# Cross-attention in seven-product blocks: product 2 of y, itself made by seven smaller products

## The chip, the cores and the metric

The kernel runs on one NeuronCore of one Trainium2 chip. The metric is the device time of one execution in microseconds (us). Matmuls run on TensorE (PE; its weight loads are recorded apart, as PEld), elementwise work on VectorE (DVE) and ScalarE (ACT), reductions over partitions on GpSimd (POOL). SyncE (SP) only issues DMAs, ACT and POOL issue a few. Each engine works through its own instructions in their order; where one needs the result of another engine, it waits on a semaphore.

## What is computed

For each of 8 batches, with C = 512 channels, N = 1024 positions and D = 64, all in float32:

```python
q = jnp.einsum('bcn,dc->bnd', x1, Wq) + bq
k = jnp.einsum('bcn,dc->bdn', x2, Wk) + bk[:, None]
v = jnp.einsum('bcn,dc->bdn', x2, Wv) + bv[:, None]
attn = jax.nn.softmax(jnp.einsum('bnd,bdm->bnm', q, k), axis=2)
attn_out = jnp.einsum('bcm,bnm->bcn', v, attn)
return attn_out + x1
```

`x1` is `x` (8, 512, 1024) and `x2` is `ctx_2048` of the same shape.

## The kernel before

Let e be the exponentials of the scores, 1024 (m) by 1024 (n), not yet divided by their sums. The kernel computes y = x2 e (512 by 1024) divided by the sums of the columns, and then out = Wv y + bv + x1. Both products are made from 2 by 2 blocks with the seven-product form of block multiplication (Winograd's variant of Strassen's): seven block products for eight, at the price of sums and differences of blocks. Blocks of the left factor (x2 transposed, called `a`, or the weights `w`) are `11`, `12`, `21`, `22`, with the sums S1 to S4; blocks of the right factor (`e`, called `t`, or `y`) have the sums T1 to T4. `MULT` (line 270) says for each product which left and right blocks it takes, into which pair of PSUM banks (`a` or `c`) it goes, and whether it opens them; otherwise it adds to what is there. Partial sums that are needed alone are copied out of PSUM by ACT into `tmp` on the way (products 1, 6, 5).

`multiply` (line 280) makes one block product. For y it is two halves j of 128 rows, each of four matmuls (contraction 4 x 128) with a moving operand of 128x512. A float32 matmul shows in the trace as two MATMUL and two LDWEIGHTS instructions, so such a product is 16 MATMULs. For out (`second`) a block product has half the contraction: 8 MATMULs.

`period` (line 442) is one batch `s` and, woven into it, the preparation of the next one, `n`. The order of the work is written out by hand; each engine follows the order of this code. PE's order in a period is: first(1), first(2), first(6) for y; the scores of the first half of `n` and the projection to queries; first(5), first(7), first(3); the scores of the second half of `n` and the keys; first(4); and then second(1), (6), (2), (5), (7), (3), (4) for out.

DVE has, among others, these steps in a period:

- `sum_e` "T1", "T2", "T4", "T3" (line 256): differences of blocks of e, each in two steps of 128x1024 elements. T3 is written in place, T4 has a buffer of its own (`eT4`).
- `evict_y` "11", step 1 (line 305): adds product 2 in bank pair `c` to the copy of product 1.
- `sums` (line 345): adds up e over the rows of blocks; `total` (line 215) then has POOL reduce it over partitions to `den`; two small DMAs and a reciprocal in `shares` (line 224) turn it into the factors for y.
- `fold` "max", `highest`, `exponentials` (lines 197, 210, 238): maximum over the scores of `n`, subtraction, and ACT's Exp.
- `sum_a` (line 127): S1 to S4 of `n`. S4 = `12` - S2 is made after first(3) of `s` (line 512); in the first period all four are made at the end of the period (lines 539 and 546).
- `evict_o` (line 330): adds bias, x1 and copies to the products of out, and SP sends the tile away.

The buffers: `a12`, `a11`, the S tiles, both e tiles and the T tiles are single; `a21` and `a22` are double. `load_a` (line 120) issues the loads of the blocks of `n` from SP, in the order of the code with all other loads and stores of SP. In PSUM there are the four banks `a0`, `a1`, `c0`, `c1`, and two double banks `sc` for scores and projections; the third of four scores uses bank pair `c` (first half) or `a` (second half).

In the first period (`s.b == 0`) things lie otherwise: the second half of the exponentials of batch 1 is made after first(1), and T4 after first(2).

Of the kernel before, what the change touches and what calls it, by code (L numbers as in the profile page):

```python
# [9 lines left out]
F32 = mybir.dt.float32  # L10
AF = mybir.ActivationFunctionType
ALU = mybir.AluOpType
# [3 lines left out]
def kernel(  # L16
# [8 lines left out]
    bv: bass.AP,  # L25
    out: bass.AP,
):

# [26 lines left out]
    nc = tc.nc  # L57
    P = 128
# [3 lines left out]
    H = 512  # L62
    MH = N // P // 2
# [4 lines left out]
    sb = ctx.enter_context(tc.tile_pool(name="sb", bufs=1))  # L68
# [3 lines left out]
    ps_s = ctx.enter_context(  # L72
        tc.tile_pool(name="ps_s", bufs=2, space=bass.MemoryType.PSUM)
    )
    ps_a = ctx.enter_context(
        tc.tile_pool(name="ps_a", bufs=1, space=bass.MemoryType.PSUM)
    )
# [6 lines left out]
    w = {  # L84
        k: const.tile([P, 2, C // 2], F32, name=f"w_{k}")
        for k in ("11", "12", "21", "22", "S1", "S2", "S4")
    }
# [6 lines left out]
    def left_sums(a, *ks):  # L94

        for k in ks:
            x, y, op = {
                "S1": ("21", "22", ALU.add),
                "S2": ("S1", "11", ALU.subtract),
                "S3": ("11", "21", ALU.subtract),  # L100
                "S4": ("12", "S2", ALU.subtract),
            }[k]
            nc.vector.tensor_tensor(a["21" if k == "S3" else k], a[x], a[y], op)  # L103
            if k == "S3":
                a["S3"] = a["21"]

    class Batch:
        def __init__(self, b):
            self.b = b
            self.a, self.e, self.t, self.y, self.o = {}, {}, {}, {}, {}  # L110
            self.mx, self.top, self.den, self.few, self.rden = {}, {}, {}, {}, {}
            self.tmp, self.bank = {}, {}

    def load_x(s, x):

        s.x = sb.tile([P, CT, N], F32, tag="x", name=f"x_{s.b}_{x.tensor.name}")
        for c in range(CT):
            nc.sync.dma_start(s.x[:, c, :], x[s.b, ts(c, P), :])  # L118
# [8 lines left out]
    def sum_a(s, *ks):  # L127
        for k in ks:
            if k != "S3":
                s.a[k] = sb.tile([P, MH, C // 2], F32, tag=f"a{k}", name=f"a{k}_{s.b}")  # L130
        left_sums(s.a, *ks)

    def project(s, nm, w_sb, bank=None):

        if bank:
            ps = ps_a.tile([P, H], F32, tag=bank, name=f"ps_{nm}_{s.b}")
        else:
            ps = ps_s.tile([P, 2, H], F32, tag="sc", name=f"ps_{nm}_{s.b}")[:, 0, :]
        for c in range(CT):
            for h, r in ((0, lo), (1, hi)):  # L140
                nc.tensor.matmul(  # L141
                    ps[r, :],
                    w_sb[:, c, :],
                    s.x[:, c, ts(h, H)],
                    start=(c == 0),
                    stop=(c == CT - 1),
                )
        return ps
# [12 lines left out]
    def keys(s, bank=None):  # L161

        ps = project(s, "k", wk_sb, bank)
        s.k = sb.tile([P, H], F32, tag="k", name=f"k_{s.b}", bufs=2)
        nc.scalar.activation(s.k, ps, AF.Identity, bias=bk_sb)  # L165
# [58 lines left out]
    def shares(s, h):  # L224

        nc.vector.reciprocal(s.few[h], s.few[h])  # L226
        row = dram.tile([1, H], F32, tag="row", name=f"row_{s.b}_{h}")
        nc.gpsimd.dma_start(row.rearrange("o (p f) -> (o p) f", p=P), s.few[h])
        s.rden[h] = s.den[h]
        nc.gpsimd.dma_start(s.rden[h], row.broadcast_to([P, H]))  # L230
# [16 lines left out]
        nc.vector.tensor_tensor(t[k], t[x], t[y], ALU.subtract)  # L247

    def open_t(s):
        for n in ("T1", "T2", "T4"):  # L250
            s.t[n] = sb.tile([P, MH, H], F32, tag=f"e{n}", name=f"e{n}_{s.b}")
        e0, e1 = s.e[0], s.e[1]
        s.t |= {"11": e0[:, 0], "12": e1[:, 0], "21": e0[:, 1], "22": e1[:, 1]}
        s.t["T3"] = s.t["12"]

    def sum_e(s, *ks):
        for i in (0, 2):
            part = {n: v[:, i : i + 2, :] for n, v in s.t.items()}
            for k in ks:
                right_sums(part, k)  # L260

    def sum_y(s, k):
# [7 lines left out]
    MULT = {  # L270
        1: ("11", "11", "a", True),
        2: ("12", "21", "c", True),
        6: ("S2", "T2", "a", False),
        7: ("S3", "T3", "c", True),
        5: ("S1", "T1", "a", False),
        3: ("S4", "22", "a", False),
        4: ("22", "T4", "c", False),
    }

    def multiply(s, stage, i, left, right, n_k):  # L280

        ka, kb, bank, opens = MULT[i]
        for j in range(2):
# [14 lines left out]
            if i in (1, 6, 5):  # L298
                s.tmp[i, j] = sb.tile([P, H], F32, tag=f"u{i}{j}", name=f"u{stage}{i}{j}_{s.b}")
                nc.scalar.copy(s.tmp[i, j], ps)  # L300


    RESULT = {"11": ("c", 1), "22": ("c", 5), "12": ("a", None), "21": ("c", 6)}

    def evict_y(s, k, steps=(1, 2)):

        bank, add = RESULT[k]
        rden = s.rden.get(int(k[1]) - 1)
        if 1 in steps:
            s.y[k] = sb.tile([P, 2, H], F32, tag=f"y{k}", name=f"y{k}_{s.b}")  # L310
        y = s.y[k]
        for step in steps:
            for j in range(2):
                ps = s.bank[bank, j]
                if add is None:
                    if step == 1:
                        nc.vector.tensor_tensor(y[:, j, :], ps, rden, ALU.mult)
                elif step == 1:
                    nc.vector.tensor_tensor(y[:, j, :], ps, s.tmp[add, j], ALU.add)  # L319
                else:  # L320
                    nc.vector.tensor_tensor(y[:, j, :], y[:, j, :], rden, ALU.mult)  # L321
# [23 lines left out]
    def sums(s, h):  # L345
        for i in range(1, MH):
            fold(s, h, i, "sum", ALU.add)
        total(s, h)
# [93 lines left out]
    def period(s, n, nn, nnn):  # L442

        def first(i):
            multiply(s, "y", i, s.a, s.t, MH)

        def second(i):
            multiply(s, "o", i, w, s.y, 2)  # L450

        open_t(s)
        first(1)
        if s.b == 0:
            head_second(s, n)
        sum_e(s, "T1", "T2")
        if s.b == 0:
            total(s, 0)
        else:
            sum_e(s, "T4")  # L460
        if n:
            load_a(n, "11")
        first(2)
        evict_y(s, "11", (1,))
        if s.b == 0:
            keys(n)
            load_x(nn, x1)
            sum_e(s, "T4")
        sums(s, 1)
        if s.b == 0:  # L470
            shares(s, 0)
        sum_e(s, "T3")
        if n:
            load_a(n, "12", "21", "22")
        first(6)

        def next_queries():
            queries(nn)
            load_x(nn, x2)

        def next_keys():
            keys(nn)
            if nnn:
                load_x(nnn, x1)

        if n:
            scores_and(n, 0, "c", next_queries if nn else nothing)
            for i in range(1, MH):
                fold(n, 0, i, "max", ALU.max)
            highest(n, 0)  # L490
        shares(s, 1)
        evict_y(s, "11", (2,))
        first(5)
        fetch_o(s, "11")
        fetch_o(s, "22")
        if n:
            for i in range(MH):
                exponentials(n, 0, i)
            if s.b:
                sum_a(n, "S1", "S2", "S3")  # L500
        first(7)
        evict_y(s, "22")
        first(3)
        evict_y(s, "12")
        if n:
            scores_and(n, 1, "a", next_keys if nn else nothing)
            sums(n, 0)
        sum_y(s, "T1")
        sum_y(s, "T2")
        if n:  # L510
            if s.b:
                sum_a(n, "S4")
            else:
                left_sums(w, "S1", "S2", "S3", "S4")
            for i in range(1, MH):
                fold(n, 1, i, "max", ALU.max)
            highest(n, 1)
            shares(n, 0)
        first(4)
        evict_y(s, "21")  # L520
        second(1)
        sum_y(s, "T3")
        sum_y(s, "T4")
        second(6)
        fetch_o(s, "12")
        if n:
            exponentials(n, 1, 0)
            exponentials(n, 1, 1)
        second(2)
        evict_o(s, "11")  # L530
        fetch_o(s, "21")
        second(5)
        if n:
            exponentials(n, 1, 2)
            exponentials(n, 1, 3)
        second(7)
        evict_o(s, "22")
        if s.b == 0:
            sum_a(n, "S1", "S2")
        if n:  # L540
            second(3)
            evict_o(s, "12")
            second(4)
            evict_o(s, "21")
            if s.b == 0:
                sum_a(n, "S3", "S4")
        else:
            second(4)
            evict_o(s, "21")
            second(3)  # L550
            evict_o(s, "12")
# [37 lines left out]
```

## Time and profile before

Three runs took 715.5, 716.59 and 716.72 us; the median is 716.59. The profile is of one execution.

| what | value |
|---|---|
| time of the profiled execution | 715.5 us |
| its span, first to last instruction | 713.7 us |
| granted TensorE clock | 1.000 |
| MATMUL and LDWEIGHTS instructions | 1892 each |
| MATMULs of line 290 (both seven-product forms), mean of one | 592 to 598 ns |
| ACT copies of 128x512 from PSUM (line 300), mean | 588 ns for y, 586 ns for out |
| ACT copies of 128x1024 (line 192), mean | 1027 ns |
| DVE steps of 128x1024 (line 241), mean | 1219 ns |
| DVE steps of 128x512 on PSUM (line 319), mean | 683 ns |
| POOL reductions of den, mean | 4079 ns |
| DMA moved | 91.67 MB, mean 128 GB/s |

The records of matmuls overlap, since they are pipelined: 592 ns is the duration of one, not the distance from one to the next. In the timeline lines that follow the columns are: start, duration of the stretch, engine, line and operation, output and inputs, shapes and count; in brackets the idle time of the engine before it and what ended it. Idle time of an engine that is not the bottleneck costs nothing by itself.

### The profile page before, as it was taken

To read this page: it belongs to the slowest core of one execution; us is meant where nothing else is said; L and a number is where in the kernel's file an instruction comes from. 1 tells how busy PE (TensorE), PEld (TensorE's weight loads), DVE (VectorE), ACT (ScalarE), POOL (GpSimd) and SP (SyncE) were. 2 spreads that over 40 slices of the span, in tenths; PEclk is the share of its full clock that TensorE was granted. 3 is DMA by queue.
4 is the path that set the end of the run, shared out by engine and by line. 5 is a ranking of instruction groups with operands and counts; after the bars stand their busy time and mean duration, and the time that the engine had idled before them with its cause. 6 is when DMAs were issued, how large, how long until landed. Compare 5 with 4: busy or idle time off the path is not lost.

```text
span 713.7 us, 5497 instructions
## 1 busy us (share of the span) xinstructions
PE 704.5 (99%) x1892; PEld 299.5 (42%) x1892; DVE 546.6 (77%) x569; ACT 200.1 (28%) x271; POOL 124.1 (17%) x86
## 2 busy tenths in 40 slices
PE   8999999999999999999999999999999999999997
PEld 4333444433444434444344443443434444444443
DVE  0998798896877968778787777778788698987254
ACT  2733412053221522124231232403224034220010
POOL 0133140031301221021210212103121040402100
PEclk9999999999999999999999999999999999999999
DMA  8577334451443614336133263332702240042003
GB/s 330 214 226 260 104 147 133 147 156 51 162 148 118 196 27 153 142 118 206 67 129 130 104 206 112 109 118 91 234 1 81 111 177 15 10 168 73 15 1 147
DMA packets 37004, 91.67 MB, mean 128 GB/s; under 512 B 5232, under 2 KB 5232, under 8 KB 36976
## 3 DMA queue, kind: packets, MB, share of 16 engines
q1 hardware_dynamic: 33344, 84.95, 33.6%
q0 software_dynamic: 2368, 4.27, 2.6%
q10 hardware_dynamic: 1264, 2.10, 0.9%
q8 instruction: 15, 0.25, 0.2%
q14 instruction: 13, 0.11, 0.1%
HBM read 72.62 MB, written 16.81 MB: 125 GB/s over the span
## 4 chain that ended last, share of the span: by engine, by line
PE 95%; DMA 2%; DVE 1%; SPq 1%; ACT 0%; issue 0%; DVEq 0%; ACTq 0%
PE ps_ya L290 31%; PE ps_yc L290 22%; PE ps_oa L290 15%; PE ps_oc L290 12%; PE ps_s L183 6%; PE ps_q L141 4%; PE ps_k L141 3%; DMA x_head<-in_x_dram 1%; DMA x_in_x_dram<-in_x_dram 1%; PE ps_sa L183 1%; PE ps_sc L183 1%; DVE aS L103 0%; DVE max L204 0%; SPq L388 0%; SPq L118 0%
## 5 line engine op out<-in xcount | busy, mean ns | idle before, releaser
L218 POOL PARTITION_ALL_REDUCE den<-sum x16 | 65.3, 4079 | 377.0 <-DVE sum L208 372.2
L290 PE MATMUL ps_ya<-eT,aS 128*128 128x512 f32 x256 | 113.1, 595 | 0.0
L290 PE MATMUL ps_yc<-e,a 128*128 128x512 f32 x256 | 112.6, 592 | 0.0
L300 ACT COPY uy<-ps_ya 128x512 f32<-128x512 f32 x48 | 28.1, 588 | 232.6 <-PE ps_ya L290 232.6
L290 PEld LDWEIGHTS ps_ya<-eT,aS 128*128 128x128 f32 x256 | 48.0, 190 | 63.8 <-issue 63.6
L290 PEld LDWEIGHTS ps_yc<-e,a 128*128 128x128 f32 x256 | 48.6, 190 | 61.6 <-issue 59.9
L241 DVE TENSOR_TENSOR e<-e,top 128x1024 f32<-128x1024 f32 x60 | 70.0, 1219 | 1.4 <-POOL top L213 1.4
L319 DVE TENSOR_TENSOR y<-ps_yc,uy 128x512 f32<-128x512 f32 x48 | 32.0, 683 | 48.6 <-PE ps_yc L290 48.6
L242 ACT ACTIVATE e<-e 128x1024 f32<-128x1024 f32 x60 | 60.9, 1052 | 18.4 <-DVE e L241 17.0
L192 ACT COPY e<-ps_s 128x1024 f32<-128x1024 f32 x47 | 46.7, 1027 | 67.8 <-PE ps_s L183 67.7
L335 DVE SCALAR_TENSOR_TENSOR o<-ps_oc,bv_sb,o 128x512 f32<-128x512 f32 x48 | 35.8, 750 | 38.9 <-PE ps_oc L290 38.9
L300 ACT COPY uo<-ps_oa 128x512 f32<-128x512 f32 x48 | 28.1, 586 | 130.7 <-PE ps_oa L290 129.4
L290 PE MATMUL ps_oc<-y,w 128*128 128x512 f32 x128 | 57.5, 592 | 0.0
L290 PE MATMUL ps_oa<-yT,w_S 128*128 128x512 f32 x128 | 57.5, 592 | 0.0
L290 PE MATMUL ps_ya<-e,a 128*128 128x512 f32 x128 | 56.3, 593 | 0.8 <-ACT e L236 0.8
L290 PE MATMUL ps_yc<-eT,a 128*128 128x512 f32 x128 | 57.0, 598 | 0.0
L290 PE MATMUL ps_ya<-e,aS 128*128 128x512 f32 x128 | 56.2, 592 | 0.0
L213 POOL PARTITION_ALL_REDUCE top<-max x16 | 32.8, 2047 | 95.6 <-DVE few L226 47.9
L183 PE MATMUL ps_s<-q,k 64*128 64x512 f32 x188 | 47.7, 608 | 1.6 <-ACT k L165 0.8
L204 DVE TENSOR_TENSOR max<-max,e 128x1024 f32<-128x1024 f32 x32 | 39.2, 1225 | 3.7 <-ACT e L190 0.5
L204 DVE TENSOR_TENSOR sum<-sum,e 128x1024 f32<-128x1024 f32 x32 | 39.2, 1225 | 2.5 <-ACT e L192 0.5
L321 DVE TENSOR_TENSOR y<-y,den 128x512 f32<-128x512 f32 x48 | 35.7, 786 | 4.8 <-DMA den<-row 4.8
(68 smaller groups left out, 755.3 us busy)
## 6 DMA issues: line engine op xcount, KB each, us to landing
x_in_x_dram<-in_x_dram SPq DMA_DIRECT2D x56, 512.0 KB, 5.8
a<-in_x2T_dram SPq DMA_DIRECT2D x32, 512.0 KB, 4.6
o<-in_x_dram SPq DMA_DIRECT2D x64, 256.0 KB, 6.1
out_dram<-o SPq DMA_DIRECT2D x64, 256.0 KB, 2.0
x_head<-in_x_dram SPq DMA_DIRECT2D x8, 512.0 KB, 8.0
den<-row POOLq DMA_DIRECT2D x16, 256.0 KB, 3.6
q<-q ACTq DMA_DIRECT2D x14, 128.0 KB, 6.9
w<-in_wvT_dram SPq DMA_DIRECT2D x4, 256.0 KB, 8.9
```

What stands on the lines that cost most here:

```text
L141: nc.tensor.matmul(ps[r, :], w_sb[:, c, :], s.x[:, c, ts(h, H)], start=(c == 0), stop=(c == CT - 1),)
L183: nc.tensor.matmul(ps[g], s.k[r, ts(i, P)], s.q[r, ts(h, H)], start=True, stop=True)
L192: nc.scalar.copy(e[:, :, i, :], whole)
L204: nc.vector.tensor_tensor(f, e[:, :, 0, :] if i == 1 else f, new, op)
L213: nc.gpsimd.partition_all_reduce(s.top[h], s.mx[h][:, 0, :], P, ReduceOp.max)
L218: nc.gpsimd.partition_all_reduce(s.den[h], s.mx[h][:, 0, :], P, ReduceOp.add)
L241: nc.vector.tensor_tensor(e, e, top, ALU.subtract)
L242: nc.scalar.activation(e, e, AF.Exp)
L290: nc.tensor.matmul(ps, left[ka][:, k, ts(j, P)], right[kb][:, k, :], start=opens and k == 0, stop=i in (2, 3, 4) and k == n_k - 1, skip_gr ...
L300: nc.scalar.copy(s.tmp[i, j], ps)
L321: nc.vector.tensor_tensor(y[:, j, :], y[:, j, :], rden, ALU.mult)
L335: nc.vector.scalar_tensor_tensor(o, s.bank[bank, j], bv_sb[:, c : c + 1], o, ALU.add, ALU.add)
```

## The change

In every period but the first, product 2 of y (`12` of x2 times `21` of e) is no longer made by `multiply`. It is cut into 2 by 2 blocks once more and made by the same seven-product form: `inner_left` and `inner_right` make four sums of each factor on DVE, `multiply_inner` makes the seven inner products, each of two matmuls with a moving operand of 128x256, and `evict_inner` adds the parts to the copies of product 1, which gives `y` "11". The inner sums of the left side lie in the buffer of S4 (`aS4`), those of the right side in the buffer of T4 (`eT4`). So T4 and S4 of the outer form are made later, after the inner products: `sum_t4` and `sum_a` "S4" now stand behind `evict_inner`, and `sums(s, 1)` before it. The inner copies use the buffers `u50`, `u51` of product 5, and the PSUM tiles `c0`, `c1` and one `sc`.

```diff
     def open_t(s):
-        for n in ("T1", "T2", "T4"):
+        for n in ("T1", "T2"):
             s.t[n] = sb.tile([P, MH, H], F32, tag=f"e{n}", name=f"e{n}_{s.b}")
...
+    def sum_t4(s):
+        s.t["T4"] = sb.tile([P, MH, H], F32, tag="eT4", name=f"eT4_{s.b}")
+        sum_e(s, "T4")
...
+    def inner_left(s):
+        x = s.a["12"]
+        v = {
+            f"{p + 1}{q + 1}": x[:, ts(q, MH // 2), ts(p, P)] for p in range(2) for q in range(2)
+        }
+        sums = sb.tile([P, 4, MH // 2, P], F32, tag="aS4", name=f"aI_{s.b}")
...
+            v[k] = sums[:, i]
+            nc.vector.tensor_tensor(v[k], v[x], v[y], op)
+        s.inner["a"] = v
+
+    def inner_right(s):
+        x = s.e[0][:, 1]
...
+        sums = sb.tile([P, 4, MH // 2, H // 2], F32, tag="eT4", name=f"eI_{s.b}")
+        for i, k in enumerate(("T1", "T2", "T3", "T4")):
+            v[k] = sums[:, i]
+            x, y = {"T1": ("12", "11"), "T2": ("22", "T1"), "T3": ("22", "12"), "T4": ("21", "T2")}[k]
+            nc.vector.tensor_tensor(v[k], v[x], v[y], ALU.subtract)
+        s.inner["t"] = v
+
+    def multiply_inner(s):
+        a, t = s.inner["a"], s.inner["t"]
+        half = [P, H // 2]
+        chain = ps_a.tile(half, F32, tag="c0", name=f"ps_i0_{s.b}")
+        second = ps_a.tile(half, F32, tag="c1", name=f"ps_i1_{s.b}")
+        third = ps_s.tile([P, 2, H], F32, tag="sc", name=f"ps_i2_{s.b}")[:, 0, 0 : H // 2]
+        u = sb.tile([P, 2, H // 2], F32, tag="u50", name=f"i6_{s.b}")
+        w = sb.tile([P, 2, H // 2], F32, tag="u51", name=f"i1_{s.b}")
+        for i, ps, copy in (
+            (1, chain, w[:, 0, :]),
+            (2, second, None),
+            (6, chain, u[:, 0, :]),
+            (7, third, w[:, 1, :]),
+            (5, chain, u[:, 1, :]),
+            (4, third, None),
+            (3, chain, None),
+        ):
+            ka, kb, _, _ = MULT[i]
+            for k in range(MH // 2):
+                nc.tensor.matmul(
+                    ps,
+                    a[ka][:, k, :],
+                    t[kb][:, k, :],
+                    start=i in (1, 2, 7) and k == 0,
...
+            if copy is not None:
+                nc.scalar.copy(copy, ps)
...
+    def evict_inner(s):
+        chain, second, third = s.inner["ps"]
+        u, w = s.inner["u"]
+        u0, u1 = s.tmp[1, 0], s.tmp[1, 1]
+        left, right = slice(0, H // 2), slice(H // 2, H)
+        s.y["11"] = y = sb.tile([P, 2, H], F32, tag="y11", name=f"y11_{s.b}")
+        for out, x, z in (
+            (u0[:, left], u0[:, left], w[:, 0, :]),
+            (y[:, 0, left], second, u0[:, left]),
+            (u1, u1, u.rearrange("p a n -> p (a n)")),
+            (y[:, 1, right], w[:, 1, :], u1[:, right]),
+            (y[:, 1, left], third, u1[:, left]),
+            (y[:, 0, right], chain, u0[:, right]),
+        ):
+            nc.vector.tensor_tensor(out, x, z, ALU.add)
...
         sum_e(s, "T1", "T2")
         if s.b == 0:
             total(s, 0)
-        else:
-            sum_e(s, "T4")
         if n:
             load_a(n, "11")
-        first(2)
-        evict_y(s, "11", (1,))
         if s.b == 0:
+            first(2)
+            evict_y(s, "11", (1,))
             keys(n)
             load_x(nn, x1)
-            sum_e(s, "T4")
-        sums(s, 1)
-        if s.b == 0:
+            sum_t4(s)
+            sums(s, 1)
             shares(s, 0)
+        else:
+            multiply_inner(s)
+            sums(s, 1)
+            evict_inner(s)
+            sum_t4(s)
+            sum_a(s, "S4")
         sum_e(s, "T3")
         if n:
             load_a(n, "12", "21", "22")
...
         if n:
             if s.b:
-                sum_a(n, "S4")
+                inner_left(n)
             else:
                 left_sums(w, "S1", "S2", "S3", "S4")
...
         evict_o(s, "22")
         if s.b == 0:
             sum_a(n, "S1", "S2")
+        elif n:
+            inner_right(n)
         if n:
             second(3)
             evict_o(s, "12")
             second(4)
             evict_o(s, "21")
             if s.b == 0:
-                sum_a(n, "S3", "S4")
+                sum_a(n, "S3")
+                inner_left(n)
+                inner_right(n)
```

More of the change, by code (lines that the diff above doesn't have):

```diff
@@ L112, in __init__ @@
             self.tmp, self.bank = {}, {}
+            self.inner = {}
     def load_x(s, x):
@@ L300, in multiply @@
                 nc.scalar.copy(s.tmp[i, j], ps)
+    def inner_left(s):
[4 more added lines that the diff above has]
+        sums = sb.tile([P, 4, MH // 2, P], F32, tag="aS4", name=f"aI_{s.b}")
+        for i, (k, x, y, op) in enumerate(
+            (
+                ("S1", "21", "22", ALU.add),
+                ("S2", "S1", "11", ALU.subtract),
+                ("S3", "11", "21", ALU.subtract),
+                ("S4", "12", "S2", ALU.subtract),
+            )
+        ):
+            v[k] = sums[:, i]
+            nc.vector.tensor_tensor(v[k], v[x], v[y], op)
+        s.inner["a"] = v
@@ new lines, in inner_right @@
+    def inner_right(s):
+        x = s.e[0][:, 1]
+        v = {
+            f"{q + 1}{r + 1}": x[:, ts(q, MH // 2), ts(r, H // 2)]
+            for q in range(2)
+            for r in range(2)
+        }
+        sums = sb.tile([P, 4, MH // 2, H // 2], F32, tag="eT4", name=f"eI_{s.b}")
[4 more added lines that the diff above has]
+        s.inner["t"] = v
@@ new lines, in multiply_inner @@
+    def multiply_inner(s):
[22 more added lines that the diff above has]
+                    start=i in (1, 2, 7) and k == 0,
+                    stop=i in (2, 3, 4) and k == MH // 2 - 1,
+                    skip_group_check=True,
+                )
+            if copy is not None:
+                nc.scalar.copy(copy, ps)
+        s.inner["ps"] = chain, second, third
+        s.inner["u"] = u, w
@@ new lines, in evict_inner @@
+    def evict_inner(s):
[11 more added lines that the diff above has]
+            (y[:, 0, right], chain, u0[:, right]),
+        ):
+            nc.vector.tensor_tensor(out, x, z, ALU.add)
@@ L313, in evict_y @@
             for j in range(2):
-                ps = s.bank[bank, j]
+                ps = s.bank.get((bank, j))
                 if add is None:
```

## The prediction

> **What bounds the kernel now.** I read the page first (busy time, then the chain that ended last), and then the timeline of one middle period, engine by engine.
>
> ```profile
> PE 704.5 (99%) x1892; PEld 299.5 (42%) x1892; DVE 546.6 (77%) x569; ACT 200.1 (28%) x271; POOL 124.1 (17%) x86
> ...
> PE 95%; DMA 2%; DVE 1%; SPq 1%; ACT 0%; issue 0%; DVEq 0%; ACTq 0%
> ```
>
> TensorE is busy for 99% of the span and is 95% of the chain. A busy PE need not be PE at its peak, so its pace has to be seen as well:
>
> ```profile
> 296.47 7.03 PE L290 MATMUL ps_ya<-e,a 128*128 128x512 f32 x16
> 303.34 7.03 PE L290 MATMUL ps_yc<-e,a 128*128 128x512 f32 x16
> 310.21 7.03 PE L290 MATMUL ps_ya<-eT,aS 128*128 128x512 f32 x16
> 317.17 1.99 PE L183 MATMUL ps_s<-q,k 64*128 64x512 f32 x8
> ```
>
> These are first(1), first(2), first(6) and the scores of the next batch. Product 2 starts at 303.34 and its successor at 310.21, so it holds PE for 6.87 us: eight matmuls recorded as 16 instructions, 0.429 us each, with no gap at either end. PE waits for nobody here, so PE time that is removed is time gained, unless a new wait eats it.
>
> **What the Trainium skill says.** "TensorE: Matmul & The Clock Gate", section "Back-to-back issue gap": at full clock a matmul instruction costs its columns at 2.4 GHz and about 2.5 ns more. With two passes of 512 columns that is 426.7 + 2.5 = 429 ns; the trace has 429. The same page, section "LDWEIGHTS (loading the stationary operand)": a load costs its columns at 1.2 GHz, 107 ns for 128, whatever the rows. The trace records 190 ns for a load, but where a load isn't hidden two loads fit in 0.30 us, so the second starts 0.11 us after the first: this agrees as a pace. "ScalarE: Activation LUTs", section "Rules for kernel authors", has about 0.83 ns an element; the trace's copies (1027 ns for 1024 columns, 588 for 512) give 0.86 ns and 0.15 us fixed.
>
> **The matmuls.** From batch 2 on is s.b = 1 to 7, seven periods. Each loses the 16 instructions of product 2 (6.87 us) and gets seven inner products of two matmuls with 256 columns: 14 matmuls, 28 instructions. Their rate isn't in the trace. By 512 columns taking 426.7 + 2.7 ns, 256 columns take 213.3 + 2.7 = 216 ns (an estimate from the page and the row above), so 28 x 0.216 = 6.05 us. Gain 0.82 us a period, 5.75 us in seven. It becomes zero at 6.87 / 28 = 245 ns an instruction. What could raise the rate is the weight load: half as many columns must hide as many loads.
>
> ```profile
> 303.34 0.19 PEld L290 LDWEIGHTS ps_yc<-e,a 128*128 128x128 f32 x1 [0.24 <-issue]
> ...
> 324.38 0.30 PEld L290 LDWEIGHTS ps_ya<-eT,aS 128*128 128x128 f32 x2 [0.81 <-issue]
> ...
> L384 PEld LDWEIGHTS ps_warm<-warm x20: 192/333/333, 1.0 to 4.7; 128*128 128x128 f32 x20
> L384 PE MATMUL ps_warm<-warm x20: 274/421/580, 1.0 to 4.8; 128*128 128x128 f32 x20
> ```
>
> A load starts with the matmul before it and lasts 190 ns, inside 216. And the warm-up did 20 loads and 20 matmuls of 128 columns with starts from 1.0 to 4.8: 3.8 / 19 = 0.20 us a pair. Whatever set that pace, load and issue allow at least 0.20 us, and 0.216 holds.
>
> **The new waits of PE.** The inner products run 1, 2, 6, 7, 5, 4, 3, of 0.864 us each. Products 6, 5 and 3 add to the bank of 1, 6, 5, and 4 to that of 7, and each must wait until ACT has copied the bank. In between lies exactly one product.
>
> ```profile
> 300.16 0.59 ACT L300 COPY uy<-ps_ya 128x512 f32<-128x512 f32 x1 [11.25 <-PE ps_ya L290]
> 303.59 0.59 ACT L300 COPY uy<-ps_ya 128x512 f32<-128x512 f32 x1 [2.85 <-PE ps_ya L290]
> 313.88 0.59 ACT L300 COPY uy<-ps_ya 128x512 f32<-128x512 f32 x1 [9.70 <-PE ps_ya L290]
> ```
>
> The first half of first(1) streams until 296.47 + 3.435 = 299.905, and its copy starts at 300.16: 0.255 us later. A copy of 256 columns should last 0.15 + 256 x 0.86 = 0.37 us. From ACT's end to PE's start the head shows 0.04 (the keys end at 14.41 on the chain, the scores start at 14.45). Sum 0.665 us against 0.864. The weight load wants to start 0.216 before its matmul, at 0.648: some 0.02 late. ACT is free: only the copy at 303.59 lies there, and it ends at 304.18, 0.28 before the first inner copy. Behind a waiting matmul stand all later ones of PE's queue. Bounds: nothing, since a load paced at 0.107 still fits, and 0.11 to 0.21 us for each of four waits, if the load comes bare and up to 0.1 late: 28 waits, 3.1 to 5.9 us. I take 0.02 us each, 0.56 us in all.
>
> **VectorE in a middle period.** The end of the period and the start of the next:
>
> ```profile
> 290.47 1.28 DVE L342 TENSOR_TENSOR o<-o,uo 128x512 f32<-128x512 f32 x2
> 291.68 0.74 DVE L335 SCALAR_TENSOR_TENSOR o<-ps_oa,bv_sb,o 128x512 f32<-128x512 f32 x1
> ...
> 296.67 0.75 DVE L335 SCALAR_TENSOR_TENSOR o<-ps_oc,bv_sb,o 128x512 f32<-128x512 f32 x1 [0.96 <-PE ps_oc L290]
> ...
> 307.04 0.69 DVE L319 TENSOR_TENSOR y<-ps_yc,uy 128x512 f32<-128x512 f32 x1 [1.36 <-PE ps_yc L290]
> 310.48 0.69 DVE L319 TENSOR_TENSOR y<-ps_yc,uy 128x512 f32<-128x512 f32 x1 [2.74 <-PE ps_yc L290]
> ...
> 315.46 4.40 DVE L247 TENSOR_TENSOR e<-e 128x1024 f32<-128x1024 f32 x2
> ```
>
> Steps follow each other on DVE every 0.60 us for 512 elements and 1.15 for 1024, plus 0.1 where one reads the one before; 256 would be 0.33 (an estimate from these). inner_right, four steps of 512, is 2.5 us and starts at 291.68. So evict_o "12" frees its first bank at 294.9 in place of 292.4; first(1) needs it at 296.47. The evictions of "21" wait for PE until 296.67, so the delay is gone there: cost nothing, with 1.6 us of cover. inner_left, four steps of 256, takes 1.4 us where S4 took 1.2: nothing.
>
> Next period: T1 and T2 still end at 303.35; the sums (3.77 + 0.6 us) now follow at once and end at 307.7; evict_inner, six steps, is 2.45 us, and the last needs the end of inner product 3 at 303.34 + 6.05 + 0.25 = 309.65. The all-reduce of den (4.13 us of POOL) goes from 315.6 to 307.9. It slowed T3 (4.40 us for two against 2.3), so I charge the same 2 us to evict_inner and T4. Then evict_inner ends near 311.2, T4 at 313.8, S4 at 315.0, T3 at 317.4. T3 ended at 319.9, or 319.1 with PE's gain taken off: DVE loses the two idle stretches of 1.36 and 2.74 us and isn't late. T4 now has a deadline: it reads the half of e that the first score copy overwrites (318.37 before, 317.5 after): 3.7 us to spare.
>
> **Queues.** On SP the loads of a "12", "21", "22" now wait for S4, 315.0 in place of 310.2. Behind them stand the x loads, which wait for the queries anyway (324.5), and the o fetches (326.5). The loads land in 4.6 us, near 321.5; their reader, S1, starts at 331.8. inner_left reads a "12" at 355. On POOL the den reduction and its two small DMAs come 7.7 us earlier. All of it is hidden.
>
> **The second batch, once.** After the first period DVE has no slack. S3 starts at 124.68 and S4 at 125.81; in S4's place come inner_left and inner_right, 3.9 us for 1.14. So T1 starts at 129.7 (126.95 before), T2 ends at 134.5 (first(6) needs it at 135.5), the sums end at 138.9, evict_inner at 142.3, T4 at 145.0. The first score copy, due at 143.7, must wait; the fourth scores wait for its bank, which was free 0.45 us early. Stall about 0.9 us; bounds 0 and 2.
>
> **The sum.** -5.75 + 0.56 + 0.9 = -4.3 us. The profiled execution took 715.5 (span 713.7 and 1.8 around it), so it would be 711.2. It is the fastest of the three shown; against their median, 716.59, the forecast is 712.3.
>
> **Rivals.**
> A, the forecast, with stalls from none to twice those above: 710 to 714. Chance 0.71.
> B, the copies are late: all 28 waits cost 0.11 to 0.21 us. For it: the margin of 0.02 us is smaller than what I know of a short copy. Against: the trace's waits on ACT that are met in time cost nothing. Time 712.3 - 0.56 + 3.1 to 5.9 = 714.8 to 717.6. Chance 0.17.
> C, the other side: weight loads set PE's pace in the inner products. If pairs run at the 0.30 us of bare loads, a period gets 28 x 0.30 = 8.4 us for 6.87, seven times +1.53 = +10.7, with the second batch 716.59 + 10.7 + 0.9 = 728. It decides from 245 ns an instruction on. Against: the warm-up's 0.20. Chance 0.06.
> D, VectorE comes later than I work out and T4 holds up the score copies in every period: steps of 256 at the price of 512 (+1.65 us) and twice the loss to POOL (+2) use up the 3.7 us; 0.5 us beyond that is 3.5 us in seven periods, time 715.8. Against: two idle stretches that vanish. Chance 0.06.
>
> **How the numbers follow.** Measurement tells 0.2%, 1.4 us, from no change. Faster by more (below 715.15): A, a third of B, a third of D: 0.71 + 0.06 + 0.02 = 0.79, and 0.02 more for mixtures of small stalls. Within: a good part of B and D, 0.09. Slower: C and B's tail, 0.10. The range runs from the full gain on the fastest run (715.5 - 5.75 = 709.75) into B, 715.8.
>
> **What would show it.** PE's start-to-start time from the first inner product to first(6): 6.05 us right, 6.5 or more means B or C. Inner instructions at 0.216 with gaps at the starts of 6, 5, 4, 3 are B; evenly slower ones are C. The score copies in the second batch wait for DVE T4, in later batches for PE. T3's end must come no later than before.

## The result and the profile after

The changed kernel takes 712.0 us (median of 4 runs, 711.94 to 712.45), the kernel before 716.05 in its 4 runs: ratio 0.9945, interval 0.9928 to 0.9962. The profiled execution after took 711.94 us with a span of 710.2, against 715.5 and 713.7 before. The forecast was 712.3.

The same two views of the page come first, busy time and the chain that ended last:

```profile
PE 700.5 (99%) x1976; PEld 315.8 (44%) x1976; DVE 576.9 (81%) x653; ACT 210.7 (30%) x299; POOL 118.4 (17%) x86
...
PE 85%; DVE 8%; DMA 4%; POOL 1%; issue 1%; ACT 1%; SPq 0%; DVEq 0%; ACTq 0%; POOLq 0%
```

TensorE has 84 matmul instructions more (12 in each of seven periods) and is still 4.0 us less busy, since the new ones have half the columns. The chain has become different in one respect: 8% of it is VectorE now. Nearly all of that lies ahead of 146.1 us: in the second batch the chain runs on VectorE from 123.4 to 146.0, and the rest is at the head and in the first period. From the scores at 147.15 on it is TensorE alone until the last evictions. The PE timeline of the middle period that the prediction showed (columns as before; the inner products are at line 365):

```profile
296.92 7.03 PE L298 MATMUL ps_ya<-e,a 128*128 128x512 f32 x16
303.79 1.89 PE L365 MATMUL ps_i<-e,a 128*128 128x256 f32 x8
305.51 2.75 PE L365 MATMUL ps_i<-eI,aI 128*128 128x256 f32 x12
308.11 1.03 PE L365 MATMUL ps_i<-eI,a 128*128 128x256 f32 x4
308.97 1.03 PE L365 MATMUL ps_i<-e,aI 128*128 128x256 f32 x4
309.83 7.03 PE L298 MATMUL ps_ya<-eT,aS 128*128 128x512 f32 x16
```

The inner products hold PE from 303.79 to 309.83, 6.04 us where product 2 held it for 6.87. Every row starts where the one before it has streamed its columns: 1.72 us for 8 instructions, 2.60 for 12, 0.86 for 4. No wait shows. In the second batch it is otherwise:

```profile
143.04 1.99 PE L187 MATMUL ps_s<-q,k 64*128 64x512 f32 x8
144.87 1.02 PE L187 MATMUL ps_sc<-q,k 64*128 64x512 f32 x4
147.15 1.13 PE L187 MATMUL ps_s<-q,k 64*128 64x512 f32 x4 [1.26 <-ACT e L196]
```

Here PE stands idle for 1.26 us ahead of the fourth scores, until ACT has copied the first. The starts of first(1) in each batch say where the time came from:

| stretch | before, us | after, us | difference |
|---|---|---|---|
| start to first(1) of batch 1 | 26.21 | 26.42 | +0.21 |
| batch 1 to batch 2 | 96.40 | 96.75 | +0.35 |
| batch 2 to batch 3 | 86.93 | 87.64 | +0.71 |
| batch 3 to batch 7, four periods | 347.73 | 344.44 | -3.29 |
| batch 7 to batch 8 | 79.76 | 79.10 | -0.66 |
| batch 8 to the end | 76.67 | 75.85 | -0.82 |

A period gains 0.82 us; the second batch gives 1.53 back. The first two rows can't be put down to the change: from first(1) of batch 1 to that of batch 2, the ten profiles of this study took 95.8 to 97.2 us, with the order there the same in all until the last steps on VectorE.

### The profile page after: what moved, and what is told of

It reads as the page before. It is cut to its first block, busy times and chain, and to the rows that moved or that the text cites. A ratio compares the mean times of both kernels' runs of the same rounds, so it can differ in the third digit from the quotient of the medians.

```text
span 710.2 us, 5772 instructions
## 1 busy us (share of the span) xinstructions
PE 700.5 (99%) x1976; PEld 315.8 (44%) x1976; DVE 576.9 (81%) x653; ACT 210.7 (30%) x299; POOL 118.4 (17%) x86
## 4 chain that ended last, share of the span: by engine, by line
PE 85%; DVE 8%; DMA 4%; POOL 1%; issue 1%; ACT 1%; SPq 0%; DVEq 0%; ACTq 0%; POOLq 0%
PE ps_ya L298 25%; PE ps_oa L298 15%; PE ps_yc L298 15%; PE ps_oc L298 12%; PE ps_i L365 5%; PE ps_s L187 5%; PE ps_k L145 3%; PE ps_q L145 3%; DVE eT L251 2%; DMA x_head<-in_x_dram 1%; DVE e L245 1%; DMA row<-few 1%; PE ps_sa L187 1%; DVE sum L208 1%; DMA x_in_x_dram<-in_x_dram 1%; PE ps_sc L187 1%
## 5 line engine op out<-in xcount | busy, mean ns | idle before, releaser
L222 POOL PARTITION_ALL_REDUCE den<-sum x16 | 59.6, 3726 | 327.2 <-DVE sum L212 322.3
L298 PE MATMUL ps_yc<-e,a 128*128 128x512 f32 x144 | 63.4, 593 | 0.0
L298 PEld LDWEIGHTS ps_yc<-e,a 128*128 128x128 f32 x144 | 27.3, 190 | 34.8 <-issue 33.1
L412 DVE TENSOR_TENSOR y<-ps_yc,uy 128x512 f32<-128x512 f32 x34 | 22.3, 679 | 24.4 <-PE ps_yc L298 24.4
```

What stands on the lines that cost most here:

```text
L222: nc.gpsimd.partition_all_reduce(s.den[h], s.mx[h][:, 0, :], P, ReduceOp.add)
L298: nc.tensor.matmul(ps, left[ka][:, k, ts(j, P)], right[kb][:, k, :], start=opens and k == 0, stop=i in (2, 3, 4) and k == n_k - 1, skip_gr ...
```

## The experiments

All are edits of the changed kernel. Four questions are asked: what the gap in the second batch waits for, whether VectorE's slack in the other periods is what was worked out, how near the ACT copies are to costing time, and what sets PE's pace at 256 columns.

**after_again**: the changed kernel, unedited, beside the next two.

> The changed kernel once more, timed on the same chip as the next two. Both theories: about 712.0 us, and in the second batch a gap of 1.3 us on PE ahead of the fourth scores.

Measured: 711.94 us (5 runs; ratio to before 0.9942, interval 0.9929 to 0.9956), with the gap of 1.3 us in the second batch. The baseline for what follows stands.

**t4_first_b2**: T4 and S4 ahead of the sums, in the second batch alone.

```diff
             multiply_inner(s)
-            sums(s, 1)
+            if s.b > 1:
+                sums(s, 1)
             evict_inner(s)
             sum_t4(s)
             sum_a(s, "S4")
+            if s.b == 1:
+                sums(s, 1)
```

> In the second batch alone the sums over e come after T4 and S4. Theory 'T4 is late on VectorE and holds up the first score copy': T4 ends near 139, the copy follows its scores, the gap on PE is gone, and the span is 1.3 to 1.6 us shorter than that of the changed kernel, time near 710.5. Rival 'PE waits for evict_inner to give back the PSUM banks c0 and c1, or the period is simply full of VectorE work': VectorE has the same steps, so a gap of at least 0.5 us stays, and the time stays within 0.5 us of 712.0.

Measured: 710.46 us (ratio 0.9923, interval 0.9910 to 0.9935), 1.5 us below after_again. ACT's timeline in the second batch, the changed kernel first, then this one; at the end of a line is what the engine waited for:

```profile
146.09 1.93 ACT L196 COPY e<-ps_s 128x1024 f32<-128x1024 f32 x2 [2.35 <-DVE eT L251]
```

```profile
144.60 1.93 ACT L196 COPY e<-ps_s 128x1024 f32<-128x1024 f32 x2 [0.51 <-PE ps_s L187]
```

The copy waited for a VectorE step at line 251, the differences of e (T4 is the only one in that place); with T4 made earlier it waits for its own scores, 1.20 us after they begin, and the period takes 86.11 us. VectorE's number of steps is unchanged, so a period that is simply full is ruled out. The edit makes evict_inner earlier too, so by itself it doesn't test the banks c0 and c1; the PE lines do. The third scores, which use these banks, start 1.83 us after the first in the changed kernel (144.87 - 143.04) and 1.82 here (145.22 - 143.40), so they don't wait, and the gap comes after them.

**t4_first_all**: the same order in all seven periods.

```diff
             multiply_inner(s)
-            sums(s, 1)
             evict_inner(s)
             sum_t4(s)
             sum_a(s, "S4")
+            sums(s, 1)
```

> The same order in all seven periods. Theory 'from the third batch on T4 has 3.5 us to spare, so the order doesn't matter there': the same time as with the second batch alone, near 710.5, periods of 86.1 us. Rival 'the sums, made later, push T3 and the maximum behind them so late that PE waits in later periods': T3 ends some 3 us later than in the changed kernel, periods longer than 86.3 us, and time over 711.5.

Measured: 710.26 us (ratio 0.9921, interval 0.9908 to 0.9933), the same as with the second batch alone, and the periods of batches 2 to 6 all take 86.1 us. T3 does end later: the maximum behind it starts 25.6 us after first(1) (320.85 - 295.22), in the changed kernel 23.0 (319.95 - 296.92). PE doesn't notice; later idle stretches of VectorE take it up. This version and the one before are faster than both kernels (all five times of each, 709.56 to 711.09, lie below the five of after_again, 711.22 to 712.66).

**reduce_later_b2**: in the second batch only the folding and POOL's reduction come later, the three additions stay ahead.

```diff
             multiply_inner(s)
-            sums(s, 1)
+            for i in range(1, MH):
+                fold(s, 1, i, "sum", ALU.add)
+            if s.b > 1:
+                total(s, 1)
             evict_inner(s)
             sum_t4(s)
             sum_a(s, "S4")
+            if s.b == 1:
+                total(s, 1)
```

> In the second batch alone the three additions of the sums stay ahead of evict_inner, but the last folding and POOL's all-reduce of den come after S4. Theory 'most of T4's delay there is the all-reduce on POOL, which stretches the 512-wide step of evict_inner from 0.7 to 2.2 us': that step takes 0.7 us, T4 ends 2.1 us earlier against the start of its period, and the gap on PE shrinks from 1.3 us to under 0.3. Rival 'the delay is the number of VectorE steps ahead of T4': only the folding (0.6 us) is saved, and a gap of 0.6 us or more stays.

Measured: 710.41 us (one run), no gap, a period of 86.11 us. VectorE's third step in evict_inner, which adds the copies of inner products 6 and 5, first in the changed kernel, with POOL's line beside it, then here:

```profile
140.41 2.20 DVE L393 TENSOR_TENSOR uy<-uy,i 128x512 f32<-128x512 f32 x1
142.64 0.42 DVE L393 TENSOR_TENSOR y<-i,uy 128x256 f32<-128x256 f32 x1
142.98 0.75 DVE L393 TENSOR_TENSOR y<-ps_i,uy 128x256 f32<-128x256 f32 x2
143.65 2.35 DVE L251 TENSOR_TENSOR eT<-e,eT 128x1024 f32<-128x1024 f32 x2
```

```profile
139.72 3.33 POOL L222 PARTITION_ALL_REDUCE den<-sum  x1 [32.69 <-DVE sum L212]
```

```profile
139.65 0.68 DVE L393 TENSOR_TENSOR uy<-uy,i 128x512 f32<-128x512 f32 x1
...
141.37 2.35 DVE L251 TENSOR_TENSOR eT<-e,eT 128x1024 f32<-128x1024 f32 x2
```

The reduction lasts from 139.72 to 143.05. The step that runs beside it takes 2.20 us, without it 0.68. That is 1.5 us of T4's delay, the folding 0.6 more; the rest of VectorE's order is as before, and T4 is in time: it ends at 143.72, the copy starts at 144.20. So the gap has a chain of four links: the inner sums are squeezed in ahead of the second batch (T1 starts 7.2 us after first(1), 4.3 before the change), the reduction comes to lie over evict_inner, T4 comes late, and the first copy waits for the half of e that T4 reads.

**t4_three_times**: takes away the slack in the other periods.

```diff
-        sum_e(s, "T4")
+        for _ in range(3 if s.b > 1 else 1):
+            sum_e(s, "T4")
```

> From the third batch on T4 is made three times (the same values), 4.5 us more of VectorE ahead of the score copy. Theory 'slack of 3.5 us for the copy and 0.45 us more at the fourth scores': PE gets a gap of 0.4 to 1.2 us ahead of the fourth scores in each of the five periods of batches 3 to 7, 2 to 6 us more in all, 714 to 718. Rival 'T4 isn't what the copy waits for in these periods': no gap there, and less than 1 us more.

Measured: 716.74 us, one run. PE in the same middle period:

```profile
317.79 1.99 PE L187 MATMUL ps_s<-q,k 64*128 64x512 f32 x8
319.61 1.02 PE L187 MATMUL ps_sc<-q,k 64*128 64x512 f32 x4
321.31 1.13 PE L187 MATMUL ps_s<-q,k 64*128 64x512 f32 x4 [0.68 <-ACT e L196]
```

The gap of 0.68 us lies inside what was expected; with the weight load that then comes bare (no running matmul hides it), periods of 87.06 us are 0.95 longer, 4.75 us in five. The slack of some 3.5 us is real, and the same mechanism waits behind it.

**copies_twice**: makes the inner copies later.

```diff
             if copy is not None:
                 nc.scalar.copy(copy, ps)
+                nc.scalar.copy(copy, ps)
```

> ACT makes each of the four inner copies twice, so that a bank is given back some 0.28 us later: 0.255 + 0.28 + 0.37 + 0.04 = 0.945 us after its product, where the product in between lasts 0.864. Theory 'the waits are met with about 0.2 us to spare, and the load of the waiting product needs only its 0.11 us': each of four waits costs 0.05 to 0.2 us, the inner products take 6.25 to 6.85 us in place of 6.05, and the time rises by 1.4 to 5.6 us. Rival 'PE doesn't wait for the copies in time at all that the trace could show, the margin is over 0.3 us': the inner products stay at 6.05 to 6.1 us.

Measured: 715.67 us, beside 715.53 for the kernel before (one run each), and periods of 86.92 us beside 86.93: the whole gain is gone. PE's weight loads, then ACT's copies, in a middle period:

```profile
305.33 1.59 PEld L365 LDWEIGHTS ps_i<-eI,aI 128*128 128x128 f32 x8 [0.40 <-ACT i L375]
307.32 0.73 PEld L365 LDWEIGHTS ps_i<-eI,aI 128*128 128x128 f32 x4 [0.40 <-ACT i L375]
308.19 0.73 PEld L365 LDWEIGHTS ps_i<-eI,a 128*128 128x128 f32 x4
309.32 0.73 PEld L365 LDWEIGHTS ps_i<-e,aI 128*128 128x128 f32 x4 [0.40 <-ACT i L375]
```

```profile
304.50 0.37 ACT L374 COPY i<-ps_i 128x256 f32<-128x256 f32 x1 [0.22 <-PE ps_i L365]
304.91 0.37 ACT L375 COPY i<-ps_i 128x256 f32<-128x256 f32 x1
```

Three times in a period a late load holds up PE: ahead of products 6, 5 and 3. The load of product 4 is 0.11 us late as well (308.19, where the spacing of 0.216 would put it at 308.08), but its matmul starts on time, at 308.29. The second copy of product 1 ends at 305.28, and product 6 starts 0.05 later, at 305.33 in place of 305.17. The inner products take 6.85 us (303.44 to 310.29), 0.80 more, so a missed wait costs 0.27 us: 0.16 of lateness at the first, and the 0.11 of a load that nothing hides. A copy that comes 0.41 us later (304.91 - 304.50) undoes the change.

**columns_split**: twice the loads for the same columns.

```diff
-                nc.tensor.matmul(
-                    ps,
-                    a[ka][:, k, :],
-                    t[kb][:, k, :],
+                for part in range(2):
+                    nc.tensor.matmul(
+                        ps[:, ts(part, P)],
+                        a[ka][:, k, :],
+                        t[kb][:, k, ts(part, P)],
```

Both halves open the PSUM tile here, and the result is no longer the product; the number of columns is the same, and only the pace of the instructions is asked about.

> Each inner matmul of 256 columns is made as two of 128, so the array streams the same columns with twice the loads: 56 MATMULs. Theory 'columns set the pace, and a load only needs 0.11 us': 56 x (0.1067 + 0.0027) = 6.1 to 6.3 us for the inner products. Rival 'a load blocks the next for its recorded 0.19 us, and 256 columns were just enough': 56 x 0.19 = 10.6 us, some 32 us more in seven periods.

Measured: 712.7 us, one run; the inner products last 6.25 us (303.48 to 309.73). PE and its loads:

```profile
303.48 1.95 PE L366 MATMUL ps_i<-e,a 128*128 128x128 f32 x16
...
309.73 1.45 PE L298 MATMUL ps_ya<-eT,aS 128*128 128x512 f32 x3
```

```profile
303.48 1.75 PEld L366 LDWEIGHTS ps_i<-e,a 128*128 128x128 f32 x15 [0.24 <-issue]
305.15 2.76 PEld L366 LDWEIGHTS ps_i<-eI,aI 128*128 128x128 f32 x24
```

56 instructions in 6.25 us are 0.112 us each, with a load for every one. The loads overlap one another: 24 of them, 192 ns each on average, fill 2.76 us and not 4.6. So the recorded 190 ns is not a load's pace, and at 256 columns (0.216 us an instruction) the loads are far from setting it.

**plain_product**: VectorE's inner sums and new order without the new matmuls; evict_inner and ACT's inner copies go with the matmuls.

```diff
-            multiply_inner(s)
+            first(2)
             sums(s, 1)
-            evict_inner(s)
+            evict_y(s, "11", (1,))
             sum_t4(s)
             sum_a(s, "S4")
```

> The new order and the eight inner sums on VectorE stay (the sums are made and not read), but product 2 is made plainly again by eight matmuls of 512 columns. Theory 'the matmuls bring 5.8 us, the rest of the change costs only the gap in the second batch': periods of 86.93 us as before the change, a gap of 0.5 to 1.5 us in the second batch, time 716 to 717.5. Rival 'the new order on VectorE also brings time, as it takes out idle stretches': periods shorter than 86.8 us and a time below 715.

Measured: 715.54 us beside 715.53 for the kernel before (one run each), periods of 86.93 us. In these periods the eight inner sums and the new order cost nothing and bring nothing; the whole gain is PE's. Only the period of batch 7 is longer, 79.93 us for 79.76. The gap that I expected isn't there: the step after the sums is then the plain eviction from PSUM, and VectorE's line for it beside the same reduction shows no stretching:

```profile
138.91 1.28 DVE L412 TENSOR_TENSOR y<-ps_yc,uy 128x512 f32<-128x512 f32 x2
140.10 3.43 DVE L251 TENSOR_TENSOR eT<-e,eT 128x1024 f32<-128x1024 f32 x2
```

T4 pays 1.1 us of the reduction, but ends at 143.5, before the copy at 144.42. Counted from first(1), T4 ends here at 21.0 us and the copy is due at 21.9; in the changed kernel T4 ends at 22.8 and the copy is due at 21.1. So evict_inner with its stretched step makes T4 1.8 us later, and PE's gain makes the copy due 0.8 us earlier. The expectation took the gap to stay, and was too high.

## Why the prediction was right, and where its sizes were off

**The matmuls, -5.75.** Right: 28 instructions in 6.04 us, 0.216 each, as estimated from the columns and a fixed 2.7 ns; 0.82 us a period. plain_product and columns_split carry it: without the matmuls no gain, and loads aren't what paces them. With that rival C falls.

**The waits on the copies, +0.56.** The term was too large: it came out as nothing, for two reasons. The hand-over is shorter than worked out. Product 1 has streamed its columns at 304.65 (303.79 + 0.864), and its copy is

```profile
304.85 0.37 ACT L374 COPY i<-ps_i 128x256 f32<-128x256 f32 x1 [0.22 <-PE ps_i L365]
```

It begins 0.20 us after the product, where 0.255 had been read from a product of 512 columns. With the 0.37 of the copy and the 0.05 that PE follows after it (copies_twice) that is 0.62 us for 0.665, so the load of product 6, due at 0.648, starts in its slot, at 305.30. And a load 0.02 us late would have cost nothing: that of product 4 in copies_twice is 0.11 us late, and its matmul starts on time. Rival B had the place right. Where a wait is missed, in copies_twice, it costs 0.27 us, the 0.11 of a bare load and 0.16 of lateness; B had the same two terms with less lateness, 0.11 to 0.21. The changed kernel misses none.

**VectorE in a middle period, 0.** Right. Against the start of first(1), 0.45 us later in this profile, T3 ends where it was put: 317.4 + 0.45 = 317.85 for a measured 318.0; T4 0.4 later than forecast, with 3.4 us to spare for 3.7. t4_three_times tests this from the other side. Rival D is the mechanism of the second batch, and it acts only there.

One step that the prediction put at nothing, inner_left, costs time in one period. The period that gains 0.66 in place of 0.82 is that of batch 7, which still prepares batch 8 but has no more queries and keys to project. Without the keys PE comes from the last scores to out 3.6 us sooner. Its weight loads for second(2), which read y "21", in the changed kernel and then in plain_product:

```profile
617.07 0.30 PEld L298 LDWEIGHTS ps_oc<-y,w 128*128 128x128 f32 x2 [0.72 <-DVE y L414]
```

```profile
619.84 0.30 PEld L298 LDWEIGHTS ps_oc<-y,w 128*128 128x128 f32 x2 [0.73 <-DVE y L414]
```

They wait for VectorE's last step on that block. Ahead of it lie inner_left's four steps, 1.46 us (609.10 to 610.56) where S4 took 1.13 (611.95 to 613.08 before). I had called inner_left hidden after looking at a period with a projection; without that cover it costs 0.16 us. PE's own gain isn't needed for it: plain_product has inner_left but not the gain, and its period of batch 7 is 0.17 us longer than before the change. That it is inner_left and no other step of the new order is read from the timelines; no run moved it alone.

**Queues, 0.** Right. SP's four loads of `a` stretch over more time and hold nobody:

```profile
303.98 13.12 SPq L129 DMA_DIRECT2D a<-in_x2T_dram  x4
```

They are issued by 317.1, and S1, their first reader, starts at 331.46 without a wait.

**The second batch, +0.9.** The mechanism was right in every link, the size too small: 1.53 us. The term that was mis-sized is evict_inner beside the reduction. I spread 1 us of the loss over it and took 3.4 us; it took 4.11 (139.54 to 143.65), as the reduction hit one step with 1.5 us. T4's own two steps, at 2.35 for 2.7, gave a little back. T4 ended 22.8 us after first(1) for 22.4 forecast, and the copy was 1.85 us late for 1.37. Another 0.11 is the bare load at the projection behind the gap.

**The sum.** -5.75 + 0 + 1.53 + 0.16 = -4.06, against -4.3 forecast: the two errors, -0.56 and +0.63, nearly cancel, beside the 0.16 that had been put at nothing. That the sum came so close is luck; that the main term fits is not. The spans differ by 3.5, because the stretch up to batch 2 took 0.56 longer in this profile; the medians differ by 4.05. With the interval of the ratio that is a gain between 2.7 and 5.2 us, so the times alone can't tell the small terms; the traces do.

## What to carry to other kernels

Where one engine is busy all the time, price a change by that engine's start-to-start pace, and then ask of every moved step which buffer it frees and who needs that buffer next: T4 was no bottleneck, it only read what a copy wanted to overwrite. The repair here was one line of order, the sums behind T4, for 1.5 us more. A reduction on POOL can be a cost to a VectorE step beside it (1.5 us here), so put a step there that nobody waits for.

## What the runs showed that I had not expected

The reduction of den doesn't slow VectorE evenly. In the changed kernel one step of 512 elements with both inputs in SBUF (the on-chip memory that the tiles lie in) took 2.20 us for 0.68, in the middle period too (309.02), where T4 has time to spare. The next step, within the last 0.4 us of the reduction, took its usual 0.42. The steps of evict_y in plain_product, which read PSUM, weren't touched, but they fell early in the reduction. What a step reads and when it falls are told apart by the shorter reductions of the maximum in the changed kernel. Two PSUM steps beside one, then two SBUF steps that start at the same distance from the start of another:

```profile
532.65 1.26 DVE L412 TENSOR_TENSOR y<-ps_yc,uy 128x512 f32<-128x512 f32 x2
533.82 1.28 DVE L414 TENSOR_TENSOR y<-y,den 128x512 f32<-128x512 f32 x2
```

```profile
532.75 1.77 POOL L217 PARTITION_ALL_REDUCE top<-max  x1 [5.33 <-DVE few L230]
```

```profile
582.89 2.10 DVE L414 TENSOR_TENSOR y<-y,den 128x512 f32<-128x512 f32 x2
```

```profile
582.99 2.20 POOL L217 PARTITION_ALL_REDUCE top<-max  x1 [12.14 <-DVE few L230]
```

At the same distance the PSUM steps take 1.26 us and the SBUF steps 2.10, and the reduction itself goes from 1.77 to 2.20. The SBUF step that starts at 533.82, 1.07 us into the first reduction, takes no longer than usual. So both count: what the step reads, and how far the reduction has come when it starts. The reduction of den, too, took 3.33 us beside evict_inner and 4.13 in reduce_later_b2, where it met T3.
